# Emitting layer 0's output projection one group of heads later

## The chip, the cores and the metric

Every run used one core of a Trainium2 chip, and each ratio compares runs of the same rounds. The metric is device time in microseconds (us). Each figure is the median of several runs, with the lowest and highest in brackets.

Names used throughout: PE is TensorE, DVE is VectorE, ACT is ScalarE, POOL is GpSimd, SP is the engine that issues the transfers (SPq L1082 in the timelines). L1190 is line 1190 of the kernel. The change adds and removes no line up to L1209, so a number up to there means the same statement in both kernels. The tiles in the profiles: e is the exponential of the scores and eb that of the bias; ps_ov holds a group's unscaled values and its softmax sums, rv is the reciprocal of these sums, gr the gate times rv, and oT the gated values that the projection ps_y reads; xo is the finished row. xt is the input, xg its group norm, lst, lmv and lrs the statistics of xg, and xn its layer norm. ps_ tiles are the kernel's PSUM tiles, the outputs of PE's groups in the profiles (L1190 PE MATMUL ps_y<-wo,oT).

## The reference, cut to what matters

```python
# x: (1, 128, 256, 256) float32: 128 rows of 256 positions of 256 channels
def layer0(m, z, ...):                      # m = groupnorm(x)
    m_norm = layer_norm(m); z_norm = layer_norm(z)
    q, k, v = m_norm @ Wq.T, m_norm @ Wk.T, m_norm @ Wv.T     # 8 heads of 32
    b = z_norm @ Wb.T                                         # bias of each pair of positions
    gate = sigmoid(m @ Wg.T + bg)
    p = softmax(q k^T / sqrt(32) + b)                         # within each row of 256
    o = (p @ v) * gate
    return o @ Wo.T + bo                                      # the output projection
x = x + layer0(groupnorm(x), ...)
x = x + layer1(groupnorm(x), ...)                             # banded attention, 4 heads
```

Only layer 0 is touched.

## The kernel before

The kernel takes the 128 rows two at a time. One pass of the outer loop is a *pair* (rows 0 and 1 of the pair, `r`), each with two *groups of heads* (`c`). While TensorE works on a pair, the generator `prep` prepares the next one, a piece at each `next(ahead)`. A group's scores are made in one step, and its values (`back`) one step later. The output projection (`finish_row`, called by `end_row`) comes one step after both groups of a row are done, so that of row 0 is made in the step `r == 1, c == 1`, and that of row 1 in the second step (`r == 0, c == 1`) of the next pair. In the built order the preparation runs further ahead than the program reads: with three xt buffers the load, xg and xn that stand in a pair belong to the pair two on.

```python
def prep(p, d):
    xt = sb.tile([P, 2 * NB, C], F32, name="xt", tag="xt", bufs=3)
    nc.sync.dma_start(xt, rows(x, s0, 2))                     # L1082: the load
    xg = sb.tile(...)
    gn_apply(xg, xt, M0, R0)                                  # POOL, L900 and L901
    nc.gpsimd.tensor_tensor(xt, xt, bcast(bo_r, 1, 2 * NB), ALU.add)   # POOL, L1085
    d["xb"] = xt                                              # xt lives on for the residual
    ...                                                       # lst (DVE), lrs (POOL L1095), xn (DVE L1098)
    yield
    ...                                                       # transposes, gate/q/k projections
    for r in range(2):
        ps = mm("ps_v")                                       # 8 matmuls, L1133
        nc.vector.tensor_tensor(v[:, r, :, :], ps..., bcast(vb_r, 1, NB), ALU.add)   # L1137
        yield

def scores(d, r, c):
    ...                                                       # 16 matmuls, exp on ACT
    eng = nc.vector if a == 0 else nc.gpsimd
    eng.tensor_tensor(e, e, eb[:, h : h + 2], ALU.mult)       # L1162, one half on each engine

def apply_values(d, r, c, es):
    ...                                                       # ps_ov, L1174
    nc.vector.reciprocal(rv[:, r, c, :], o[:, 1, :])          # L1179
    ...                                                       # gr
    nc.vector.tensor_tensor(d["oT"][:, c, :], o[:, 0, :], gr, ALU.mult)   # L1184

def finish_row(d, r, xo):
    ps = mm("ps_y")                                           # pool of two with ps_v, ps_x, ps_p
    ...                                                       # 8 matmuls, L1190
    nc.vector.tensor_tensor(xo, ps..., d["xb"][:, r * NB : (r + 1) * NB, :], ALU.add)   # L1194: reads xt

for p in range(NP):                                           # ... (cut)
    for r in range(2):
        for c in range(KC):
            es = scores(d, r, c)
            next(ahead, None)
            end_row()                                         # output projection
            next(ahead, None)
            back()                                            # values of the group before
            next(ahead, None)
            todo = (d, r, c, es)
```

Every fourth pair (eight rows) also makes the group-norm statistics for layer 1: 32 statistics instructions and a merge of small DVE operations (L862 to L869).

## Time and profile before

| | before |
|---|---|
| time of the first three runs | 5007.69 us (5001.58 to 5008.73) |
| PE busy over the whole span | 90% |
| idle time of PE before the output projection | 286.5 us |
| spacing of loads, plain pair / every fourth pair | 36.7 / 43.7 us (means of 45 and 15) |

From the page of the kernel before: its span, the busy time of the engines, and the output projection's group (busy us and mean ns of one | idle us before it, and what ended most of it).

```profile
span 5000.1 us, 78757 instructions
...
PE 4524.3 (90%) x30240; PEld 2915.0 (58%) x30240; DVE 2864.0 (57%) x8095; ACT 1936.3 (39%) x5014; POOL 2114.3 (42%) x1264
...
L1190 PE MATMUL ps_y<-wo,oT 128*128 128x256 f32 x1024 | 309.5, 443 | 286.5 <-DVE oT L1184 286.4
```

The last line: 286 us of idle TensorE, all before one instruction group, all put down to oT. The mean of 443 ns for one matmul hides a second cost: in the x8 group at 1515.78, at a granted clock of 1.00, the mean is 379 ns, and in the x6 group at 1537.98, after a wait and at a clock of 0.56, it is 620 ns. So groups that follow a wait can run slow as well.

### The profile page before, as it was taken

What the parts mean: (1) busy time and instruction counts of PE and PEld (TensorE: products, weight loads), DVE (VectorE), ACT (ScalarE), POOL (GpSimd) and SP (SyncE); (2) the same over time, 40 slices, a digit from 0 to 9 for tenths busy, and PEclk for the clock granted to TensorE, in tenths of its full rate; (3) what the DMA queues carried; (4) which work ended last, traced back from release to release, by engine and by line L of the source; (5) the groups of instructions that cost most, each with busy time, mean ns of one, the idle gap of its engine ahead of it and who ended that gap; (6) DMA issues with size and microseconds to landing.
All of it is one profiled execution on the core that took longest, in us unless ns stands there. A gap on an engine that the chain in (4) does not pass through costs nothing.

```text
span 5000.1 us, 78757 instructions
## 1 busy us (share of the span) xinstructions
PE 4524.3 (90%) x30240; PEld 2915.0 (58%) x30240; DVE 2864.0 (57%) x8095; ACT 1936.3 (39%) x5014; POOL 2114.3 (42%) x1264
## 2 busy tenths in 40 slices
PE   5787988889888898888898869999999999999999
PEld 5785554445444554554454436666666666666666
DVE  7875677776777777777767743333333333333333
ACT  1122333333333333333333324444444444444444
POOL 2334444444444445444444433333333333333332
PEclk9999999999999999999999989999999999999999
DMA  6630010000000010001001011111111111111100
GB/s 221 209 131 13 14 35 31 31 31 19 30 31 31 31 35 14 31 31 35 31 14 35 27 40 35 35 35 35 35 35 35 35 35 35 35 35 35 34 32 27
DMA packets 189236, 211.47 MB, mean 42 GB/s; under 512 B 5936, under 2 KB 171824, under 8 KB 188720
## 3 DMA queue, kind: packets, MB, share of 16 engines
q1 hardware_dynamic: 188848, 206.33, 12.3%
q8 instruction: 239, 3.92, 0.3%
q14 instruction: 149, 1.22, 0.1%
HBM read 138.16 MB, written 68.16 MB: 41 GB/s over the span
## 4 chain that ended last, share of the span: by engine, by line
PE 56%; DVE 19%; POOL 9%; DMA 3%; issue 2%; ACT 1%; ACTq 0%; SPq 0%; POOLq 0%; DVEq 0%
PE ps_p L1329 9%; PE ps_sc L1379 6%; PE ps_o L1435 5%; PE ps_ov L1174 5%; PE ps_y L1444 5%; PE ps_v L1344 4%; DVE rv L1179 4%; DVE xn L1098 3%; DMA xt<-in_x_dram 3%; PE ps_v L1133 3%; PE ps_pt L1420 3%; PE ps_y L1190 3%; POOL xg L901 2%; PE ps_vm L1355 2%; PE ps_o L1436 2%; POOL xg L900 2%
## 5 line engine op out<-in xcount | busy, mean ns | idle before, releaser
L1162 POOL TENSOR_TENSOR e<-e,eb 128x1024 f32<-128x1024 f32 x256 | 652.6, 2549 | 1033.0 <-ACT e L1159 1033.0
L1159 ACT ACTIVATE e<-ps_sc 128x1024 f32<-128x1024 f32 x512 | 496.6, 1022 | 883.6 <-PE ps_sc L1150 883.5
L1408 POOL TENSOR_TENSOR e<-e,rw 112x512 f32<-112x512 f32 x256 | 266.4, 1041 | 1220.3 <-DVE rm L1407 691.5
L1179 DVE RECIPROCAL rv<-ps_ov 128x256 f32<-128x256 f32 x256 | 448.4, 1752 | 233.9 <-PE ps_ov L1174 233.2
L1397 ACT ACTIVATE e<-t,nmx 112x128 f32<-112x128 f32 x1024 | 398.1, 389 | 441.5 <-DVE nmx L1389 432.3
L1190 PE MATMUL ps_y<-wo,oT 128*128 128x256 f32 x1024 | 309.5, 443 | 286.5 <-DVE oT L1184 286.4
L1329 PE MATMUL ps_p<-xgT,w_in 128*128 128x512 f32 x1024 | 474.4, 606 | 0.0
L1190 PEld LDWEIGHTS ps_y<-wo,oT 128*128 128x128 f32 x1024 | 213.4, 215 | 375.7 <-DVE oT L1184 284.1
L900 POOL TENSOR_TENSOR xg<-xt,M_l 128x1024 f32<-128x1024 f32 x128 | 300.5, 2347 | 185.6 <-DMA xt<-in_x_dram 164.5
L1389 DVE CUSTOM_DVE_ANT_0 t<-ps_sc,bw 112x128 f32<-112x128 f32 x1024 | 253.0, 281 | 176.3 <-PE ps_sc L1379 170.6
L1162 DVE TENSOR_TENSOR e<-e,eb 128x1024 f32<-128x1024 f32 x256 | 317.0, 1238 | 24.9 <-ACT e L1159 24.9
L1379 PE MATMUL ps_sc<-kT,qT 64*112 64x128 f32 (+1 forms) x3072 | 328.1, 274 | 0.4 <-DVE nmm L1393 0.4
L1425 ACT COPY eT<-ps_pt 128x448 f32<-128x448 f32 x256 | 136.2, 532 | 470.9 <-PE ps_pt L1422 453.5
L901 POOL TENSOR_TENSOR xg<-xg,R_l 128x1024 f32<-128x1024 f32 x128 | 309.6, 2419 | 10.0
L1435 PE MATMUL ps_o<-eT,v 128*64 128x112 f32 x2048 | 307.7, 273 | 0.0
L1329 PEld LDWEIGHTS ps_p<-xgT,w_in 128*128 128x128 f32 x1024 | 179.6, 190 | 201.5 <-issue 124.0
L1133 PE MATMUL ps_v<-wv,xnT 128*128 128x256 f32 x1024 | 292.9, 436 | 2.6 <-DVE v L1137 2.6
L1150 PE MATMUL ps_sc<-qT,kT 32*128 32x256 f32 x4096 | 294.4, 400 | 0.0
L1174 PE MATMUL ps_ov<-e,v 128*32 128x256 f32 x4096 | 274.2, 385 | 0.0
L1174 PE MATMUL ps_ov<-e,ones 128*32 128x256 f32 x4096 | 267.9, 379 | 0.0
L1150 PEld LDWEIGHTS ps_sc<-qT,kT 32*128 32x128 f32 x4096 | 185.6, 184 | 139.4 <-issue 133.8
L1133 PEld LDWEIGHTS ps_v<-wv,xnT 128*128 128x128 f32 x1024 | 218.1, 222 | 77.8 <-DVE v L1137 22.5
(157 smaller groups left out, 8484.6 us busy)
## 6 DMA issues: line engine op xcount, KB each, us to landing
xa<-in_x_dram SPq DMA_DIRECT2D x8, 4096.0 KB
xt<-in_x_dram SPq DMA_DIRECT2D x64, 512.0 KB
x<-xo SPq DMA_DIRECT2D x16, 2048.0 KB
xt<-x SPq DMA_DIRECT2D x64, 512.0 KB
out_dram<-yo SPq DMA_DIRECT2D x64, 512.0 KB
rsum<-rv SPq DMA_DIRECT2D x64, 16.0 KB
rs_all<-rsum SPq DMA_DIRECT2D x1, 1024.0 KB
w_in<-in_w_inT_dram SPq DMA_DIRECT2D x1, 768.0 KB
```

Source lines behind the costliest of these rows:

```text
L900: nc.gpsimd.tensor_tensor(dst, src, bcast(M, 1, n), ALU.subtract)
L901: nc.gpsimd.tensor_tensor(dst, dst, bcast(R, 1, n), ALU.mult)
L1133: nc.tensor.matmul(ps[:, b * C : (b + 1) * C], xnT[:, k, t * P : (t + 1) * P], wv[:, k, :], start=(k == 0), stop=(k == KC - 1),)
L1150: nc.tensor.matmul(pss[q // 2][:, q % 2, b, :], d["kT"][rs, c, r * I + b * P : r * I + (b + 1) * P], d["qT"][rs, c, r * I : (r + 1) * I], ...
L1159: nc.scalar.activation(e, pss[a], AF.Exp)
L1162: eng.tensor_tensor(e, e, eb[:, h : h + 2], ALU.mult)
L1174: nc.tensor.matmul(o[q * D0 : (q + 1) * D0, what, :], w, es[q // 2][:, q % 2, b, :], start=(b == 0), stop=(b == NB - 1),)
L1179: nc.vector.reciprocal(rv[:, r, c, :], o[:, 1, :])
L1190: nc.tensor.matmul(ps[:, b * C : (b + 1) * C], d["oT"][:, k, b * P : (b + 1) * P], wo[:, k, :], start=(k == 0), stop=(k == KC - 1),)
L1329: nc.tensor.matmul(ps, w_in[:, k, n * C + m * P : n * C + (m + 1) * P], xgT[:, k, :], start=(k == 0), stop=(k == KC - 1),)
L1379: nc.tensor.matmul(pss[q][:nq, at : at + nk], d["qT"][rs, c, r * I + q0 : r * I + q0 + nq], d["kT"][rs, c, r * I + k0 : r * I + k0 + nk], ...
L1435: nc.tensor.matmul(oq[:, q0 : q0 + W], d["v"][:, r, w, hs], eT[:, q, w, :], start=True, stop=True)
```

## The change

Its intent: when ps_y comes up in TensorE's queue, oT isn't ready. Put the values of the next group and a piece of preparation ahead of ps_y, so that TensorE has something to do meanwhile. As a group's `back()` now runs before the row's end, oT needs a third buffer and is handed along.

```diff
-        def finish_row(d, r, xo):
+        def finish_row(d, r, oT, xo):
 ...
-                        ps[:, b * C : (b + 1) * C], d["oT"][:, k, b * P : (b + 1) * P], wo[:, k, :],
+                        ps[:, b * C : (b + 1) * C], oT[:, k, b * P : (b + 1) * P], wo[:, k, :],
 ...
-                d_["oT"] = sb.tile([P, KC, I], F32, name="oT", tag="oT")
+                d_["oT"] = sb.tile([P, KC, I], F32, name="oT", tag="oT", bufs=3)
 ...
-                rowend = (d_, r_, d_["p"])
+                rowend = (d_, r_, d_["p"], d_["oT"])
 ...
                     es = scores(d, r, c)
                     next(ahead, None)
-                    end_row()
+                    due = rowend
+                    back()
                     next(ahead, None)
-                    back()
+                    if due is not None:
+                        end_row(due)
                     next(ahead, None)
                     todo = (d, r, c, es)
```

(The tail after the loop ends the second-last row once more before `back()`.)

More of the change, by code (lines that the diff above doesn't have):

```diff
@@ L1214, in back, with end_row @@
             if c_ == KC - 1:
-                rowend = (d_, r_, d_["p"])
-        def end_row():
+                rowend = (d_, r_, d_["p"], d_["oT"])
+        def end_row(due):
             nonlocal rowend, xo
-            if rowend is None:
-                return
-            d_, r_, p_ = rowend
+            d_, r_, p_, oT_ = due
             s = 2 * p_ + r_
@@ L1224, in end_row @@
                 xo = sb.tile([P, GB * NB, C], F32, name="xo", tag="xo")
-            finish_row(d_, r_, xo[:, (s % GB) * NB : (s % GB + 1) * NB, :])
+            finish_row(d_, r_, oT_, xo[:, (s % GB) * NB : (s % GB + 1) * NB, :])
             if r_ == 1:
@@ L1234, in end_row @@
                 gn_merge(xo, GB * NB, st1, j, sm)
-            rowend = None
+            if rowend is due:
+                rowend = None
         for p in range(NP):
@@ L1253, in fast_kernel @@
             d = nxt
+        if rowend is not None:
+            end_row(rowend)
         back()
-        end_row()
+        end_row(rowend)
         M1, R1 = gn_finish(st1, 1, sb, ps_mm, "l1")
```

## The prediction

> **What bounds the kernel now.** I read the page first, then the table of stretches, the waits inside layer 0, and the timeline of one pair of rows. The table of stretches (PE, weight load, DVE, ACT, POOL busy, then granted clock) splits the kernel:
>
> ```profile
> 1500.00:2000.00 500.00, 439.16 (x3436) 250.83 (x3437) 363.19 (x548) 180.51 (x234) 239.16 (x105) 0.95 0.08 28
> 3500.00:5000.00 1500.00, 1489.88 (x8688) 994.31 (x8686) 538.80 (x3167) 706.94 (x2734) 573.88 (x513) 0.99 0.10 34
> ```
>
> Layer 1 (from about 3000 us) keeps TensorE at 99% and isn't touched. Layer 0 (507 to 2925 us by the first and last output projection) leaves it idle 12% of the time, at a clock of 0.95. The waits of layer 0 (600 to 2600 us) name one idle reason for PE of any size:
>
> ```profile
> PE ps_y L1190 <- DVE oT L1184: 238.1, 64, 7.7
> PE ps_v L1133 <- DVE v L1137: 2.2, 13, 0.2
> ```
>
> That is the wait which the change attacks: the output projection ps_y waits for oT, 286.5 us over the kernel by the page. The obvious reading is "move ps_y later and win up to 286 us". But the question is why oT is late. The timeline of one pair, whose scores start at 1507.90 us, answers it (start, duration, engine, line):
>
> ```profile
> 1515.78 1.89 PE L1190 MATMUL ps_y<-wo,oT 128*128 128x256 f32 x8
> ...
> 1517.71 0.69 DVE L1194 TENSOR_TENSOR xo<-ps_y,xt 128x512 f32<-128x512 f32 x1 [1.36 <-PE ps_y L1190]
> ...
> 1518.46 0.36 SPq L1082 DMA_DIRECT2D xt<-in_x_dram  x1
> ...
> 1522.10 2.35 POOL L900 TENSOR_TENSOR xg<-xt,M_l 128x1024 f32<-128x1024 f32 x1 [3.54 <-DMA xt<-in_x_dram]
> ...
> 1524.53 2.42 POOL L901 TENSOR_TENSOR xg<-xg,R_l 128x1024 f32<-128x1024 f32 x1
> ...
> 1526.91 2.38 POOL L1085 TENSOR_TENSOR xt<-xt,bo_r 128x1024 f32<-128x1024 f32 x1
> ...
> 1529.39 1.02 POOL L1095 TENSOR_TENSOR lrs<-lrs,mhalf 128x4 f32<-128x4 f32 x1
> ...
> 1530.38 2.35 POOL L1162 TENSOR_TENSOR e<-e,eb 128x1024 f32<-128x1024 f32 x1
> 1530.45 3.09 DVE L1098 TENSOR_SCALAR xn<-xg,lmv,lrs 128x256 f32<-128x256 f32 x3 [1.13 <-POOL lrs L1095]
> ...
> 1534.91 1.75 DVE L1179 RECIPROCAL rv<-ps_ov 128x256 f32<-128x256 f32 x1
> ...
> 1537.98 2.70 PE L1190 MATMUL ps_y<-wo,oT 128*128 128x256 f32 x6 [2.90 <-DVE oT L1184]
> ```
>
> The reader is to see a loop. The xt tile has three buffers. The load of the next xt starts 0.06 us after xo has read the oldest one (1518.40), so an xo of this pair starts a load; the load feeds POOL's normalisation; its result feeds xn on DVE; and DVE, in its fixed order, does the second half of row 0 (rv, gr, oT) only behind xn. That oT lets ps_y of row 0 go, and the next pair's first ps_y starts the next load. From the end of xo to the end of oT is 1537.93 - 1518.40 = 19.5 us. The period of a plain pair is set by this loop, not by TensorE's own work (about 31.8 us, the sum of its groups' spacings at full clock). Starts of the waiting ps_y group in consecutive pairs (1581.96, 1619.13, 1655.99, 1691.53, 1735.50) give 37.2, 36.9, 35.5 us for plain pairs, mean 36.5, and 44.0 for every fourth pair, where DVE also does the 32 statistics instructions and the merge.
>
> [...] after 7.73 us idle the x6 group of ps_y took 2.93 us, after shorter waits 2.70, 1.94 or 1.56. [...] rv at 1534.91 has had its matmuls finished since 1529.74 but stands behind xn. [...] three xn beside a POOL e take 3.09 us, one alone 0.40[...].
>
> **The change part by part.** No arithmetic is added or removed; the instruction order of the built kernels tells what moves.
>
> 1. PE, first half of a pair. Before: scores, xg, ov, xn, scores, wg, ps_y (starting 7.88 us after the pair). After: scores, ov, xg, xn, scores, wg, ov, wg, ps_y. One more ov (1.86) and one more wg (1.81) stand ahead, and xn directly follows xg, so about 0.25 us waits for ACT's copies. ps_y starts at about 7.9 + 3.7 + 0.25 = 11.8, and xo ends 2.62 later (as 1515.78 to 1518.40) at 14.4 instead of 10.5. The load, hence the loop, starts 3.9 us later in the pair.
> 2. PE, second half. Before: v, ps_y, v, ov. After: v, ov, v, ps_y. What was between ps_y and the next pair, v (1.83) and ov (1.86), 3.7 us, now lies ahead of it. So (1) and (2) cancel on TensorE, and the wait is still there if oT isn't earlier.
> 3. POOL. Before: L900, L901, L1085, lrs, e, e, ... After: L900, L901, L1085, e, lrs, e, ... One e of 2.35 us now stands ahead of lrs, on the loop.
> 4. DVE. Before: xn x3, e, xn, rv, gr, oT. After: e goes ahead of the statistics (into idle time), then xn, xn, rv, xn, gr, xn, oT, e, v, and only then rv of the next group.
> 5. PSUM. Behind both v groups, ps_y takes in a pool of two buffers the one that the first v group used. It therefore needs not only oT but also DVE's copy of v, which in DVE's queue stands behind oT and an e (1.21 + 0.68 us).
>
> Loop from the end of xo, plain pair: load 3.70, three POOL operations 7.2 (to 10.9), e 2.35, lrs 1.0 (14.25), two xn 2.75[...], rv 1.75, xn 0.35, gr 0.45, xn 0.35, oT 0.4 (20.3), e 1.2, v 0.7: 22.1 us. TensorE reaches ps_y at about 31 (it has also waited 1 us at the ov of row 1 for POOL's e, which ends near 27.7), and starts it at 14.4 + 22.1 = 36.6. The wait is about 5.5 us instead of 2.9. ps_y's eight at full clock take 1.73, so the next pair starts at 38.3; an idle gap of 5 us should nearly always throttle, which costs about 2.1 us, as after the 7.7 us waits: 40.4. With nine in ten throttled, 40.2, against 36.5.
>
> Every fourth pair: from the end of xo 32 statistics 6.3, e 1.2, merge 7.4, rv 1.75, gr and oT 1 to 3, statistics and lrs 3.1, xn 3.5, e and v 1.9: about 26.4; ps_y at 40.8, throttled 3.5, period 44.3 against 44.0. No gain.
>
> Sum: some 48 plain pairs x 3.7 = +178, 15 others x 0.3 = +5: about 5190 with nearly every gap throttled. If none is, 48 x 1.8 = +86 and the result is 5095. I lean to the throttled case and take 5165.
>
> **The rivals.** (a) The wait just goes: ps_y has 3.7 us of other matmuls ahead against a wait of 2.9 in plain pairs, so 48 x 2.9, part of the merge waits and some clock come back, about 4780. For it: the waits view, which shows nothing else. Against it: the loop; oT isn't bound to the place of ps_y in PE's queue but to the start of the load, which moves with ps_y. (b) A standoff: the load starts later, but POOL's and DVE's slack absorbs the extra e, and only the fast clock differs: 4980 to 5060. For it: POOL is busy under half of the stretch (239 of 500 us). Against it: its operations on the loop run back to back. (c) The loop lengthens, as worked out.
>
> **Range and chances.** (c) has nearly all my weight; its uncertain term is the clock after each gap (1.8 to 3.9 us per plain pair), then the hand-made schedule (about 1 us per pair either way, 50 us in all). Range 5080 to 5215. Slower by over 2% begins at 5107.8: 0.77. Same 0.16, faster 0.07 for a loop that I misread.
>
> **What would show it.** Right: PE's idle time before L1190 grows (to about 64 x 6 us) though ps_y stands behind other matmuls, released by DVE v L1137 rather than oT L1184; POOL e ahead of lrs; the load issued about 14 us into the pair; ov L1174 waiting about 1 us for POOL; a clock under 0.94 in 1000 to 2500; layer 1 unchanged. Wrong: idle time before L1190 that shrinks below 150 us, loads that start before xo of the pair, or periods under 36 us.

## More of the kernel before

(A run that deletes the line L1085 has all later numbers one lower.)

The spacing of the xt loads in the transfer queue is the length of a pair, read without any modelling; four loads cover eight rows.

## The result, and the profile after

| | before | after |
|---|---|---|
| time, same rounds | 5004.64 us (4999.82 to 5008.73) | 5158.93 us (5153.11 to 5166.81) |
| spacing of loads, plain pair | 36.7 us | 41.1 us |
| spacing of loads, every fourth pair | 43.7 us | 41.0 us |
| idle time of PE before the output projection | 286.5 us | 309.6 us |
| one matmul of it, mean | 443 ns | 499 ns |

The ratio is 1.031, with an interval of 1.029 to 1.033: slower. Ratios here are the mean time of one kernel's fast runs over that of the other's of the same rounds, so not quite the ratio of the quoted medians.

The page of the kernel after, the same three lines:

```profile
span 5161.6 us, 78617 instructions
...
PE 4630.3 (90%) x30240; PEld 2955.7 (57%) x30240; DVE 2710.1 (53%) x8095; ACT 1943.3 (38%) x5014; POOL 2099.2 (41%) x1264
...
L1190 PE MATMUL ps_y<-wo,oT 128*128 128x256 f32 x1024 | 348.0, 499 | 309.6 <-DVE v L1137 306.9
```

The same 30240 matmuls keep PE busy for 106 us longer (4524.3 to 4630.3): no work was added, so they ran slower. PE's idle time before ps_y didn't go; it grew by 23 us, under another releaser. Another 34 us of idle time are new before ps_ov (L1174). Much of the loss thus shows as slower matmuls after the waits rather than as waits.

The table of stretches of the kernel after (PE, weight load, DVE, ACT, POOL busy, then granted clock):

```profile
1500.00:2000.00 500.00, 431.34 (x3223) 243.59 (x3224) 310.35 (x519) 169.40 (x218) 217.25 (x96) 0.93 0.08 27
```

Every engine got less done in these 500 us than before (PE 3223 matmuls against 3436, POOL 96 operations against 105), at a clock of 0.93 against 0.95. No engine became the bound. All are slowed together, which fits a longer loop of dependencies. The waits of PE in layer 0 of the kernel after, 600 to 2600 us (total us, times, longest):

```profile
PE ps_y L1190 <- DVE v L1137: 242.0, 48, 7.5
PE ps_ov L1174 <- POOL e L1162: 25.3, 37, 0.7
```

The timeline of one plain pair of the kernel after; its first scores start at 1505.67 (start, duration, engine, line, operation, and in brackets the idle time before it with what ended it):

```profile
1518.11 1.89 PE L1190 MATMUL ps_y<-wo,oT 128*128 128x256 f32 x8
...
1520.03 0.69 DVE L1194 TENSOR_TENSOR xo<-ps_y,xt 128x512 f32<-128x512 f32 x1 [0.94 <-PE ps_y L1190]
...
1520.79 0.36 SPq L1082 DMA_DIRECT2D xt<-in_x_dram  x1
...
1524.56 2.77 POOL L900 TENSOR_TENSOR xg<-xt,M_l 128x1024 f32<-128x1024 f32 x1 [7.45 <-DMA xt<-in_x_dram]
...
1532.02 2.35 POOL L1162 TENSOR_TENSOR e<-e,eb 128x1024 f32<-128x1024 f32 x1
...
1534.33 1.02 POOL L1095 TENSOR_TENSOR lrs<-lrs,mhalf 128x4 f32<-128x4 f32 x1
...
1538.07 1.74 DVE L1179 RECIPROCAL rv<-ps_ov 128x256 f32<-128x256 f32 x1
...
1540.63 0.41 DVE L1184 TENSOR_TENSOR oT<-ps_ov,gr 128x256 f32<-128x256 f32 x1
1540.96 1.21 DVE L1162 TENSOR_TENSOR e<-e,eb 128x1024 f32<-128x1024 f32 x1
1542.10 0.68 DVE L1137 TENSOR_TENSOR v<-ps_v,vb_r 128x512 f32<-128x512 f32 x1
...
1542.83 3.06 PE L1190 MATMUL ps_y<-wo,oT 128*128 128x256 f32 x8 [4.55 <-DVE v L1137]
```

Set this beside the pair of the kernel before that the prediction shows. The ps_y of the previous pair starts 12.44 us into the pair instead of 7.88. Its xo still triggers the load within 0.07 us. POOL now does an e (1532.02) ahead of lrs (1534.33). From the end of xo (1520.72) to the oT that row 0 needs is now 20.3 us instead of 19.5, and to the copy v, which frees ps_y's PSUM buffer, 22.06 us. The projection was put 3.7 us later in TensorE's queue, and what it waits for came later still.

### The profile page after: what moved, and what is told of

It is laid out like the page before. It is cut to its first block, busy times and chain, and to the rows that moved or that the text cites. A ratio compares the mean times of both kernels' runs of the same rounds, so it can differ in the third digit from the quotient of the medians.

```text
span 5161.6 us, 78617 instructions
## 1 busy us (share of the span) xinstructions
PE 4630.3 (90%) x30240; PEld 2955.7 (57%) x30240; DVE 2710.1 (53%) x8095; ACT 1943.3 (38%) x5014; POOL 2099.2 (41%) x1264
## 4 chain that ended last, share of the span: by engine, by line
PE 62%; POOL 12%; DVE 11%; DMA 6%; issue 0%; SPq 0%; ACT 0%; POOLq 0%; DVEq 0%
PE ps_p L1332 9%; PE ps_y L1190 6%; PE ps_sc L1382 6%; DMA xt<-in_x_dram 6%; PE ps_o L1438 5%; PE ps_p L1122 5%; PE ps_ov L1174 5%; PE ps_y L1447 5%; PE ps_v L1347 4%; DVE xn L1098 4%; PE ps_sc L1150 4%; POOL xg L900 3%; PE ps_pt L1423 3%; POOL xg L901 3%; PE ps_x L1108 3%; PE ps_vm L1358 2%
## 5 line engine op out<-in xcount | busy, mean ns | idle before, releaser
L1162 POOL TENSOR_TENSOR e<-e,eb 128x1024 f32<-128x1024 f32 x256 | 621.9, 2429 | 1070.8 <-ACT e L1159 1070.8
L1190 PE MATMUL ps_y<-wo,oT 128*128 128x256 f32 x1024 | 348.0, 499 | 309.6 <-DVE v L1137 306.9
L900 POOL TENSOR_TENSOR xg<-xt,M_l 128x1024 f32<-128x1024 f32 x128 | 327.5, 2559 | 401.8 <-DMA xt<-in_x_dram 380.5
L1190 PEld LDWEIGHTS ps_y<-wo,oT 128*128 128x128 f32 x1024 | 248.0, 249 | 406.7 <-DVE v L1137 331.4
L1150 PE MATMUL ps_sc<-qT,kT 32*128 32x256 f32 x4096 | 358.8, 425 | 0.0
L1174 PE MATMUL ps_ov<-e,v 128*32 128x256 f32 x4096 | 304.2, 386 | 33.9 <-POOL e L1162 33.9
L1150 PEld LDWEIGHTS ps_sc<-qT,kT 32*128 32x128 f32 x4096 | 218.8, 202 | 168.4 <-issue 157.6
L901 POOL TENSOR_TENSOR xg<-xg,R_l 128x1024 f32<-128x1024 f32 x128 | 306.6, 2395 | 10.0
L1098 DVE TENSOR_SCALAR xn<-xg,lmv,lrs 128x256 f32<-128x256 f32 x256 | 215.0, 870 | 172.9 <-POOL lrs L1095 172.1
L1174 PE MATMUL ps_ov<-e,ones 128*32 128x256 f32 x4096 | 287.3, 379 | 0.0
L1122 PE MATMUL ps_p<-xgT,wg 128*128 128x512 f32 x512 | 256.5, 624 | 0.5 <-ACT xnT L1109 0.5
```

The costliest lines, as they stand in the source:

```text
L900: nc.gpsimd.tensor_tensor(dst, src, bcast(M, 1, n), ALU.subtract)
L901: nc.gpsimd.tensor_tensor(dst, dst, bcast(R, 1, n), ALU.mult)
L1122: nc.tensor.matmul(ps, w[:, k, m * P : (m + 1) * P], src[:, k, :], start=(k == 0), stop=(k == KC - 1))
L1150: nc.tensor.matmul(pss[q // 2][:, q % 2, b, :], d["kT"][rs, c, r * I + b * P : r * I + (b + 1) * P], d["qT"][rs, c, r * I : (r + 1) * I], ...
L1174: nc.tensor.matmul(o[q * D0 : (q + 1) * D0, what, :], w, es[q // 2][:, q % 2, b, :], start=(b == 0), stop=(b == NB - 1),)
L1190: nc.tensor.matmul(ps[:, b * C : (b + 1) * C], oT[:, k, b * P : (b + 1) * P], wo[:, k, :], start=(k == 0), stop=(k == KC - 1),)
```

## The experiments

The theory, the loop: the period of a pair is the loop "ps_y of row 1 of the pair before → xo → load into the freed xt buffer → POOL → xn → rv, oT of row 0 → ps_y of row 0 → rest of the pair → next ps_y of row 1". The change delays the loop's start as much as it delays the waiter, and lengthens the DVE and POOL part between. Three rivals stand against it. The new releaser: ps_y now needs a PSUM buffer that the v copy frees, and that by itself is the harm, whenever the load comes. The clock alone: the waits are of much the same total, but of a shape that slows more matmuls behind them. POOL's order alone: e ahead of lrs costs its 2.35 us in each pair. (In the expectations, "the loop" is the first of these.)

### One part alone: only row 0's end late, only row 1's end late

The two halves of the change do opposite things to the loop. Row 1's end starts it (its xo reads xt last). Row 0's end closes it. So `late_r0` should gain and `late_r1` lose. The edit, against the changed kernel, shown for late_r0; late_r1 has `r == 0` in place of `r == 1`:

```diff
                     due = rowend
-                    back()
+                    if due is not None and not (r == 1):
+                        end_row(due)          # row 1's end: at the old place
+                    if r == 1:
+                        back()
                     next(ahead, None)
-                    if due is not None:
+                    if not (r == 1):
+                        back()
+                    if due is not None and r == 1:
                         end_row(due)          # row 0's end: late
                     next(ahead, None)
```

> Half of the change alone: the projection of row 0 is emitted late, that of row 1 stays at its old place. In the built order POOL keeps lrs ahead of e, as before. Loop theory: xo of row 1 ends 10.5 us into the pair as before, so the load is not delayed; from there 19.5 us to oT and 1.9 to DVE's copy of v, so row 0's ps_y starts at 31.9, which TensorE reaches at about 30.3; plain pairs of 33.7 us against 36.5, every fourth about 43.4: 4840 to 4890 us, clearly faster than both kernels. Rival (the later place itself costs TensorE, half of the loss per half): about 5080. Rival (the wait simply goes with the later place): 4850 too, so this run alone does not tell that one.

Measured: 4887.45 us (4883.33 to 4889.25), ratio 0.977 (0.975 to 0.978). As expected; plain pairs take 34.2 us on average. Two places of its timeline: the load's trigger, in a pair whose scores start at 1017.76, and from its page the projection's line:

```profile
1027.73 0.69 DVE L1194 TENSOR_TENSOR xo<-ps_y,xt 128x512 f32<-128x512 f32 x1 [1.36 <-PE ps_y L1190]
1028.48 0.36 SPq L1082 DMA_DIRECT2D xt<-in_x_dram  x1
```

```profile
L1190 PE MATMUL ps_y<-wo,oT 128*128 128x256 f32 x1024 | 278.2, 419 | 145.0 <-DVE v L1137 140.7
```

The load is issued 10.7 us into the pair, as in the kernel before (10.6), and row 0's projection still stands behind 3.7 us of other matmuls: PE's idle time before it is halved. In this kernel too ps_y waits for the v copy, so the new releaser by itself isn't the harm.

> The other half alone: row 1's projection late, row 0's at its old place. In the built order POOL has e ahead of lrs and DVE has four xn ahead of rv. Loop theory: xo of row 1 ends at about 14.4 us of the pair, oT of row 0 some 20.3 us later, ps_y waits about 8 us, [...] and v and ov still follow: plain pairs of about 41.9 us, every fourth 42 to 45: 5200 to 5300 us, slower than the whole change. Rival (half of the loss per half): about 5080. Rival (a later place takes the wait away): under 5000.

Measured: 5313.49 us (5313.04 to 5314.19), ratio 1.062 (1.060 to 1.064): the direction as expected, the size slightly above its range. Its waits of PE in layer 0:

```profile
PE ps_y L1190 <- DVE oT L1184: 319.0, 46, 7.8
```

Plain pairs take 42.3 to 43.6 us (mean 42.9), and the mean clock of 1000 to 2500 us falls to 0.89 (0.94 in the kernel before). The x6 groups of ps_y at 1075.73, 1118.45 and 1161.98 waited 7.80 us and took 2.93 us each, against 1.56 us at 1655.99 in the kernel before, at a clock of 1.00. Row 1's part alone costs 313 us, row 0's part alone gains 113 us; the sum, +200, is near the whole change's +154. So the change consists of a part that helps and a part that hurts more. The halves differ in more than the load's time, though: in the built order of late_r0 POOL keeps lrs ahead of e (1039.42 and 1040.41), while in late_r1 e comes first (1066.34 and 1068.65). The 313 us therefore contain POOL's order too, and this pair of runs doesn't separate the two.

### The loop cut: a fourth buffer of xt

The idea: with four buffers the load that follows an xo serves a pair one further on (three on instead of two), so it has a pair's slack. By the loop theory the change should then cost next to nothing, while the new releaser and POOL's order stay as they are. To make room, the last range check of `eb` was moved out of layer 0's pool.

```diff
-            xt = sb.tile([P, 2 * NB, C], F32, name="xt", tag="xt", bufs=3)
+            xt = sb.tile([P, 2 * NB, C], F32, name="xt", tag="xt", bufs=4)
 ...
-        check(eb.rearrange("p h b i -> p (h b i)"), math.exp(-20.0), math.exp(20.0), 0, sb)
     with tc.tile_pool(name="chk", bufs=1) as ck, ...
 ...
+        check(eb.rearrange("p h b i -> p (h b i)"), math.exp(-20.0), math.exp(20.0), 0, ck)
```

> The kernel before with four xt buffers instead of three (room made by moving one final check to a later pool). Loop theory: the load no longer hangs on this pair's xo, so it can run a pair ahead, rv of row 0 no longer stands behind a late xn, and PE's wait at ps_y goes in plain pairs (to about 32 to 33 us), while every fourth pair keeps a part of its DVE work: 4720 to 4820 us. Rival (DVE's queue, not the load, makes oT late): within 40 us of 5005.

> The changed kernel with four xt buffers, same edit. Loop theory: the place of ps_y no longer matters for the load, so the loss of the change vanishes: 4700 to 4820 us, as fast as the kernel before with the same edit or somewhat faster. Rival (the later place itself costs, through PSUM or the order of matmuls): about 150 us above the kernel before with four buffers.

Measured: before_xt4 4747.34 us (4739.48 to 4749.1), ratio 0.948; after_xt4 4768.04 us (4764.36 to 4769.87), ratio 0.953. Both times are as expected, and the difference between the two orders shrinks from 154 to 21 us: nearly the whole cost of the change needs the loop that three buffers make. But the cut isn't the one expected. A plain pair of before_xt4, whose scores start at 1189.50:

```profile
1203.50 2.35 POOL L900 TENSOR_TENSOR xg<-xt,M_l 128x1024 f32<-128x1024 f32 x1 [2.71 <-DMA xt<-in_x_dram]
...
1211.76 1.75 DVE L1179 RECIPROCAL rv<-ps_ov 128x256 f32<-128x256 f32 x1
...
1227.27 0.54 DVE L1098 TENSOR_SCALAR xn<-xg,lmv,lrs 128x256 f32<-128x256 f32 x1
```

The load is still issued 0.06 us after an xo (1200.06) and 10.56 us into the pair, as with three buffers, and POOL still waits for it. What the built order moved is xn: it now comes in the next pair, behind rv, not ahead of it. So lrs and xn, and with them the e that the change puts ahead of lrs, are off the path, and from the end of xo to the end of oT it is 15.8 us instead of 19.5. Two rivals thus stay untested by these runs. Buffer count and DVE's order changed together: three buffers with xn placed behind oT wasn't run. And POOL's order can cost nothing here, so it is tested below, not by this pair. The waits of PE in layer 0 with four buffers, first in the old order:

```profile
PE ps_y L1190 <- DVE oT L1184: 95.6, 29, 4.5
```

and in the new:

```profile
PE ps_y L1190 <- DVE v L1137: 30.6, 15, 3.0
```

With four buffers, the change does to the wait what its intent says (95.6 to 30.6 us in these 2000 us). Plain pairs take 32.2 us on average in the old order, where TensorE is busy all the time (32.00 of 32.00 us from 1061.62 on) and nothing is left to hide, and 34.3 us in the new one; every fourth pair falls from 40.3 to 35.5 us on average (34.3 to 37.3). The two nearly balance. Of the 2 us by which the new order's plain pairs are longer, the trace puts 1.3 in the ps_ov that waits for POOL's e (1088.01 to 1091.18, against 1.86 us elsewhere) and 0.6 in a stop between the transposes of xg and xn (1064.68 to 1065.30).

The control that moves the check alone:

> Control for the kernels with four xt buffers: the kernel before with three, and only the final check moved to the later pool. 4990 to 5015 us: the gain of four buffers is not the check's.

Measured: 5009.47 us, ratio 1.002 (1.001 to 1.004): the check's place is worth nothing.

### The clock alone: matmuls that fill the gap

If the clock carries a large part of the loss, work that only fills the wait must save time. The value projection of row 1 is repeated three times (same result, 8 matmuls becoming 24) just ahead of the late ps_y:

```diff
-                for b in range(NB):
+                for b in [b for _ in range(3 if r == 1 else 1) for b in range(NB)]:
```

> The changed kernel with the second value projection's matmuls of every pair written three times over (same result, each repeat starts its sum anew): 3.5 us more work for TensorE per pair, 221 us in all, just ahead of the wait. Clock theory: the 4.5 us idle gap shrinks to about 1, the clock is not throttled afterwards, and each pair gets about 2 us shorter (38.3 for 40.2): about 5035 us (5000 to 5070), faster in spite of the added work. Rival (TensorE's work is on the path): 5380. Rival (the gap's length is all that counts and the clock costs nothing): 5155.

Measured: 5066.66 us (5060.31 to 5073.7), ratio 1.013 (1.011 to 1.015), within its range: 92 us less than the changed kernel although its value projections keep PE busy 221 us longer. In its timeline:

```profile
1019.84 5.45 PE L1133 MATMUL ps_v<-wv,xnT 128*128 128x256 f32 x24
...
1026.39 1.99 PE L1190 MATMUL ps_y<-wo,oT 128*128 128x256 f32 x8 [1.10 <-DVE v L1137]
```

The group after the wait takes 1.99 us, not 3.06 to 3.78, and the mean clock of the whole kernel is 0.99. Plain pairs take 39.1 us on average instead of 41.1, every fourth 39.9 instead of 41.0: this part is the clock, some 2 us a plain pair. The rest (39 against 36.7) stays with the clock at 0.99, so the clock is a real part and not the whole.

### POOL's order and the bias addition

The POOL addition of `bo` (L1085, 2.35 us) lies on the loop between L901 and lrs. It's deleted here; the result stays right only because bo is zero.

```diff
-            nc.gpsimd.tensor_tensor(xt, xt, bcast(bo_r, 1, 2 * NB), ALU.add)
```

> The changed kernel without the addition of bo to xt on POOL (2.4 us per pair; the result stays right only because bo is zero in these inputs). Loop theory: that addition stands between xg and e and lrs on the loop, and lst is ready as soon as e has run, so the loop loses 2.25 us per plain pair and some throttling: 4980 to 5050 us. Rival (POOL, under half busy, is off the path): no change, 5155.

> The same removal in the kernel before. There lrs stands directly behind the addition, but waits just as long for DVE's statistics (both end at 1529.3 us in the pair shown): the loop theory expects next to nothing, 4985 to 5010 us. If removing POOL work helps both kernels alike (100 us or more here), the e ahead of lrs is not what the change added to the loop.

Measured: after_nobo 5053.15 us (5050.92 to 5056.57), ratio 1.010, just above its range; before_nobo 4961.73 us (4957.35 to 4967.26), ratio 0.992, a miss by 23 us. In the changed kernel 2.35 us taken off POOL's part of the loop shortens a plain pair by 2.1 us on average (41.06 to 38.97; two in three take 38.3 to 38.9, the others 39.5 to 40.1): POOL's operations do lie on the loop, nearly one for one. In the kernel before, the same deletion leaves plain pairs as they were (36.60 against 36.67 us on average), as expected. Only every fourth pair gains (41.9 instead of 43.7), and that is the miss: the expectation didn't look at these pairs, where gr, which takes 2.58 us beside the addition at 1570.34 in the kernel before, takes 0.44 us without it. The timeline of a plain pair of before_nobo shows why nothing is gained there:

```profile
1507.74 0.43 DVE L1089 BATCH_NORM_STATS2 lst<-xg 128x6 f32<-128x256 f32 x1 [2.25 <-POOL xg L901]
...
1510.04 1.01 POOL L1094 TENSOR_TENSOR lrs<-lrs,mhalf 128x4 f32<-128x4 f32 x1 [2.33 <-DVE lrs L1093]
```

POOL's lrs needs DVE's statistics of xg, which take from 1507.74 to 1509.97. With the addition gone POOL idles 2.33 us for them: in the old order the addition lay in that gap and was free. In the changed kernel the addition fills the gap and the e behind it is what lengthens the loop; delete the addition, and e slides into the gap. From this I infer that POOL's order is worth about 2.1 us of each plain pair of the changed kernel, and nothing without the addition; a kernel with POOL's order alone put back wasn't run. Even then plain pairs (38.97) stay 2.4 us above those of before_nobo (36.60), so POOL's order isn't the whole either.

Taken together, the filled gap took 2.0 us off a plain pair of the changed kernel and the deletion 2.1: 4.1 of the 4.4 us that the change added. No run does both, and the kernel before has slowed groups of its own, so that the two add up is not shown. It fits the prediction's points 1 and 2: the later start of the loop and the matmuls brought ahead of ps_y nearly cancel, and what is left is the longer stretch on POOL, and the clock.

### The helpful half with the loop cut, and the harmful half with the loop cut

> Row 0's projection late, row 1's at its old place, and four xt buffers. Loop theory: with the load off the path the plain pairs stay bound by TensorE at about 32.1 us (as in the kernel before with four buffers), and every fourth pair, where ps_y of row 0 has 3.7 us more matmuls ahead of DVE's merge work, falls from about 41 to 39 us: 4690 to 4740 us, the fastest of all. Rival (a late projection costs whatever the buffers): above 4760.

Measured: 4709.87 us (4709.7 to 4710.58), ratio 0.942 (0.941 to 0.944), as expected. It's the fastest of all: only row 0's projection is late, and xt has four buffers. Plain pairs take 32.2 to 32.6 us and every fourth 37.7.

> Row 1's projection late, row 0's at its old place, and four xt buffers: the worst half of the change without the loop. Loop theory: its loss of 310 us against the kernel before was the delayed load and nothing else, so it falls to the level of the other kernels with four buffers, 4720 to 4800 us. Rival (row 1's late place costs by itself): over 4900.

Measured: 4862.04 us (4859.3 to 4867.85), ratio 0.973, a miss by 62 us. With four buffers row 1's delay loses far less than its 313 us of before (it is 115 us above before_xt4), but not nothing. The timeline of one pair shows why:

```profile
1098.40 0.69 DVE L1194 TENSOR_TENSOR xo<-ps_y,xt 128x512 f32<-128x512 f32 x1 [0.93 <-PE ps_y L1190]
1099.15 0.37 SPq L1082 DMA_DIRECT2D xt<-in_x_dram  x1
...
1108.15 1.41 DVE L1090 BATCH_NORM_STATS2 lst<-xg 128x6 f32<-128x256 f32 x4 [4.68 <-POOL xg L901]
1110.37 1.74 DVE L1179 RECIPROCAL rv<-ps_ov 128x256 f32<-128x256 f32 x1
...
1113.53 1.56 PE L1190 MATMUL ps_y<-wo,oT 128*128 128x256 f32 x6 [1.54 <-DVE oT L1184]
```

The load is still issued 0.06 us after an xo, and though it now serves a pair one further on, its statistics (lst) stand in DVE's queue ahead of this pair's rv, whose matmuls had ended at about 1106.6. DVE idles 4.68 us for POOL's xg with rv behind it. So a remnant of the loop is left (xo, load, xg, lst, rv, oT: 14.4 us from the end of xo to the end of oT instead of about 20), and row 1's delay still feeds it. My expectation had overlooked that the place in DVE's queue, not only the data, ties the two together.

### What was not run

Moving the bo addition and spreading the merge over several pairs were built, but the scheduler put the instructions back in the same order, so there was nothing to run. Not tried were three buffers with xn behind oT in DVE's queue, POOL's order alone, and the filled gap together with the deleted addition.

## Why the prediction was right

The prediction named the loop and its direction, and its 5165 stands against 5158.93. The mechanism was earned, the closeness is luck in part: 5165 was set between a sum of 5190 with nearly every gap throttled and one of 5095 with none; the trace shows the throttled case (groups of 3.06 or 3.78 us behind the waits of 1500 to 1700 us, against 1.89 us without one), and two errors below cancelled. Its steps, one by one:

| step | predicted | measured |
|---|---|---|
| ps_y of the pair before starts, us into the pair | 11.8 | 12.44 |
| end of xo, us into the pair | 14.4 | 15.05 |
| end of xo to end of v copy | 22.1 us | 22.06 us |
| wait of ps_y / of ov | 5.5 / 1 us | 4.55 / 0.67 us |
| plain pair against before | +3.7 us | +4.4 us (36.67 to 41.06) |
| every fourth pair against before | +0.3 us | -2.7 us (43.71 to 41.00) |
| idle time before L1190 | about 384 us | 309.6 us |
| clock, 1000 to 2500 us | under 0.94 | 0.92, 0.93, 0.93 |

**The mechanism.** The releaser v instead of oT, POOL's e ahead of lrs, and the load tied to xo came as described. Layer 1 is unchanged (PE busy 500.00 of 500 us in 3200 to 3700). The experiments back each link: delay the start alone (with POOL's new order), and it costs 313 us; delay the end alone, and it gains 113; take lrs and xn off the loop with a fourth buffer, and the change's cost falls to 21.

**Two terms of the sum were mis-sized and cancelled.** Measured with the load spacings, 45 plain pairs times 4.40 give +198 us, and 15 fourth pairs times -2.71 give -41 us; together 157 us, against a measured difference of 154. The prediction had +178 and +5.

The plain pair was put too short by some 0.7 us, and some 0.6 us of that is the earlier ps_y's start, 12.44 us into the pair instead of 11.8. In the timeline, the stop between xg and xn, where two scores matmuls also stand, is 0.63 us (1509.79 to 1510.42) where I allowed 0.25; the first scores, behind a slow group, take 1.23 us to the next group instead of 1.07; and the first wg group 1.91 instead of 1.82. The start of the next load moves with it. (The listed terms of the loop add up to 22.2 us where the prediction wrote 22.1, and those of every fourth pair to 26.2 to 28.2, where it wrote 26.4.)

The fourth pair failed in the term "merge 7.4". I copied it from the kernel before. There the merge stands beside POOL's work, and three of its six small operations take 2.4 us, ten times what they take alone. In the kernel before:

```profile
1563.15 2.37 POOL L1162 TENSOR_TENSOR e<-e,eb 128x1024 f32<-128x1024 f32 x1 [7.73 <-ACT e L1159]
1563.22 2.41 DVE L869 TENSOR_TENSOR st<-st,gst 128x64 f32<-128x64 f32 x1
1565.48 2.37 POOL L900 TENSOR_TENSOR xg<-xt,M_l 128x1024 f32<-128x1024 f32 x1
1565.54 2.39 DVE L863 SCALAR_TENSOR_TENSOR gd<-gd 128x64 f32<-128x64 f32 x1
```

and in the kernel after:

```profile
1651.10 0.23 DVE L869 TENSOR_TENSOR st<-st,gst 128x64 f32<-128x64 f32 x1
1651.26 0.21 DVE L863 SCALAR_TENSOR_TENSOR gd<-gd 128x64 f32<-128x64 f32 x1
...
1652.55 2.36 POOL L900 TENSOR_TENSOR xg<-xt,M_l 128x1024 f32<-128x1024 f32 x1 [2.62 <-DMA xt<-in_x_dram]
```

Before, POOL's e falls due 7.9 us after the end of xo (1555.26), right as the merge begins, with xg behind it, and the slow merge operations end within 0.15 us of a POOL operation. (An xn beside a POOL e does the same in the pair that the prediction shows: of the three at 1530.45 the first took 2.44 us and ended 0.14 us after that e, the other two 0.40 us each.) After, POOL's e has run 4 us after xo, beside the statistics, and POOL then waits for its load until 1652.55; the merge (1650.94 to 1652.06) finds POOL silent and takes 1.1 us. That takes the chain from xo to v from the predicted 26.4 down to 22.6 us, though DVE then waits 1.8 us for POOL's xg. This is read from the traces; no run moved the merge alone. The nearest is before_nobo: there the three merge operations still take 2.4 us each, but gr, beside the addition before, takes 0.44 us instead of 2.58, and just these pairs gain.

**The clock's reading.** The groups of 2.70 and 1.94 us that the prediction lists followed waits of only 2.90 and 2.83 us. Waits of 2.8 to 3.0 us already slowed the group behind them in two of three plain pairs of the kernel before (six matmuls in 2.70 and 1.94 us against 1.56). In the pair that the prediction shows the clock fell only after the wait of 2.90 us had ended at 1537.98: the granted clock was 1.00 from 1537 to 1538, 0.62 in the next microsecond and 0.50 in the two after. Behind the wait of 7.73 us it read 0.50 from 1581 to 1586. That a gap of 5 us should nearly always throttle was my estimate from those 7.7 us waits; in the kernel after, the groups of eight behind waits of 4.55 and 4.56 us at 1542.83 and 1583.39 took 3.06 us at a clock of 0.63 and 3.78 us at 0.50.

**The idle time** was put too high (384) since waits of 4.6 us, not 6, occur, and more of the loss sits in slowed matmuls: PE's busy time rose by 106 us, its idle time before ps_y by only 23.

**The rivals.** (a), that the wait just goes, holds in part for half of the change (late_r0: idle time halved, 113 us gained); with four buffers the wait shrinks too, but the time doesn't. (b), a standoff, is what remains with a fourth buffer: +21 us. With three buffers both fell.

## What to carry to other kernels

Follow a wait back to what starts its producer before moving the waiter: where the producer's chain starts from the waiter's own instance one round earlier (here by a freed buffer), moving the waiter moves both ends, and here only changes that moved one end, or took work off the loop with a buffer, gained. After a change of buffers read the built order again: here the load stayed where it was, and what gained was that xn no longer stood ahead of rv in DVE's queue. Look at the count of buffers of tiles that live on for a late read, such as a residual: one more xt buffer was worth 5.2%, and with row 0's projection alone late 5.8%. And a duration copied from a profile holds only as long as the neighbours on the other engines stay where they are: the merge went from 2.4 us to 0.2 us for one operation because POOL's work moved.
